# Attention scores of two heads in one go: cross terms over all rows, both high-high terms on half of the rows each

## The chip, the cores and the metric

The kernel runs on one core of a Trainium2 chip. The metric is device microseconds from start to end of one launch. The engines that appear below are PE (TensorE: matmuls; its weight loads are listed as PEld), DVE (VectorE), ACT (ScalarE), POOL (GpSimd) and SP (SyncE, which issues transfers). Matmuls write into PSUM, the accumulator memory, from which ACT and DVE read.

## What is computed

A residual block with masked self-attention in which queries, keys and values are the same projection: 16 batches, 512 channels, 1024 tokens, 8 heads of 64. About half of the tokens are masked out.

```python
def _L0_cond_ref(x, mask, Wq, Wo):
    NH = 8
    NEG = -1e+30
    B, D, T = x.shape
    dk = D // NH
    scale = 1.0 / jnp.sqrt(jnp.asarray(dk, x.dtype))
    xt = jnp.transpose(x, (0, 2, 1))
    q = xt @ Wq.T
    qh = q.reshape(B, T, NH, dk).transpose(0, 2, 1, 3)
    scores = scale * jnp.einsum('bhqd,bhkd->bhqk', qh, qh)
    cmask = mask[:, None, None, :]
    rmask = mask[:, None, :, None]
    logits = (scores * cmask + (1.0 - cmask) * NEG) * rmask
    attn = jax.nn.softmax(logits, axis=-1)
    ctx = jnp.einsum('bhqk,bhkd->bhqd', attn, qh)
    ctx = ctx.transpose(0, 2, 1, 3).reshape(B, T, D)
    out = ctx @ Wo.T
    return jnp.transpose(out, (0, 2, 1))
x = x + _L0_cond_ref(x, cond_2048, L0_cond_Wq, L0_cond_Wo)
```

## The kernel before

Only tokens with mask 1 attend and are attended to; the others get the mean. The kernel gathers the unmasked rows of a batch into C = 544 slots (four blocks of 128 and a tail of 32), works on those, and adds the mean's projection to the other rows.

**Numbers in two halves.** A float32 value is kept as h + l, two float16 numbers, h the rounded value and l the rest. The projections (`query`, L447, and `product`, L727) multiply h.h, h.l and l.h and leave l.l out. The scores need q.q within a head. `qsplit` makes, for each pair of heads, a tile `xx` of 128 partitions with four slots of 544 columns. For the pair's first head, slot 0 holds h in partitions 0 to 63 and l in 64 to 127, and slot 1 holds l and h, the other way round. For the second head, slot 2 holds h and l, and slot 3 l and h. A matmul of slot 0 with slot 0 over all 128 rows gives h.h + l.l at once, and one of slot 0 with slot 1 gives the two cross terms h.l + l.h. Four transfers on SP's queue fill `xx` (SP, "xx<-hl").

**Scores** (`scores`, L620). One call is one head `p` and one row block `i`: four matmuls into a tile `pss` of two PSUM banks, first h.h + l.l for both halves of the columns (g = 0, 1; 272 columns each), then the cross terms for both. One exp on ACT (L624) reads the tile into `p` and sums its rows (the accumulator is read by an instruction of its own). The pool `ps_s` has two such tiles. With `i` as None the tails of four heads are done together (L595), in four column groups of 32.

**Attend** (L643). exp(scores) times v, in float32, for both heads of a pair: the first head writes PSUM partitions 0 to 63, the second 64 to 127, so each matmul takes 64 columns of the array. The sixteen matmuls of a pair of heads for its four row blocks come as one block (32 records in the trace): the first is `group_first`, and the others are queued behind it with raised priority. The tail's part (L647) ends the sum, and ACT copies it out (L651).

**The order of the work.** `run` goes through the batches; a batch has 18 steps: 4 pairs of heads x 4 row blocks, and two steps for the tails. In a step the code issues the first head's scores, then planned work (`fill`, with a share of the batch's list by cost), then the second head's scores, then transfers and, at i = 1, the attend block of the pair before, then planned work again. The planned work belongs to the batches beside this one: transposes (`xt`, L424), queries (L447), values (L497), projections (L727), sums. Costs and shares are written by hand; at i = 0, 1, 2, 3 the shares before and after the second head are (1.0, 0.6), (0.1, 0.5), (0.9, 1.0), (0.9, 0.9). The code's order is a priority: the framework's scheduler issues, on each engine, what it takes to be ready, so an instruction can go ahead of one that waits. `behind(i)` puts what is written in it behind instruction `i` on its engine, and `high_priority` moves it up. The pool `ps_m` (tiles `pm`) has two buffers for everything but scores and attends.

**Beat.** `self.beat` is the last matmul of the latest scores or query; gathers and scatters on POOL (L339, L811) and some sums on DVE wait for it, so that they come at a steady pace. `self.exp` is the last exp; the sums over x on ACT are queued behind it.

Of the kernel before, what the change touches and what calls it, by code (L numbers as in the profile page):

```python
# [10 lines left out]
F32 = mybir.dt.float32  # L11
# [3 lines left out]
AF = mybir.ActivationFunctionType  # L15
# [4 lines left out]
P = 128  # L20
D = 512
T = 1024
H = 8
DK = 64
# [3 lines left out]
SCALE = 0.125  # L28
NEG = -1.0e30

C = 544
CT = C - 512
CH = C // 2
CQ = C + 2
CM = C
HG = H // 2
# [10 lines left out]
HPO = 300  # L47


class Fast:  # L50
# [531 lines left out]
    def scores(self, b, p, i):  # L582


        nc, s = self.nc, self.st[b]
        if "z" not in s:
            s["z"] = self.sb([P, H, 4], F32, "z", 2)
            s["zt"] = self.sb([P, 2], F32, "zt", 2)
        if i is None:
            pt = self.ps_s.tile([P, 2, 512], F32, tag="s", name="pss")  # L590
            for a in range(2):
                for g in range(2):
                    for r in range(HG):
                        xx, k = s["xx"][2 * p + r // 2], r % 2
                        self.beat = nc.tensor.matmul(pt[r * CT:(r + 1) * CT, g, :CH], lhsT=xx[:, 2 * k, 512:C],  # L595
                                                     rhs=xx[:, 2 * k + a, g * CH:(g + 1) * CH],
                                                     start=(a == 0), stop=(a == 1)).ins
            t = self.sb([P, C], F32, "p", 12)
            nc.scalar.activation(t.rearrange("p (g c) -> p g c", g=2), pt[:, :, :CH], AF.Exp,  # L599
                                 bias=s["nm"][p][:, HG:], scale=SCALE, accum_out=s["zt"][:, p:p + 1])  # L600

            hi = self.sb([P, C], F32R, "c", 4)
            lo = t.bitcast(F32R)
            nc.vector.tensor_copy(hi, t)
            nc.vector.tensor_tensor(lo, t, hi.bitcast(F32), ALU.subtract)  # L605

            def spread():
                s["pt"] = self.sb([P, 2, C], F32R, "pt")
                half = slice(0, DK), slice(DK, P)
                for k in range(2):  # L610
                    nc.sync.dma_start(out=s["pt"][half[k], k, :].bitcast(F32), in_=hi[half[k]].bitcast(F32))
                    nc.sync.dma_start(out=s["pt"][half[1 - k], k, :].bitcast(F32), in_=lo[half[k]].bitcast(F32))

            self.later(spread)
            return None
        xx, k = s["xx"][p // 2], p % 2
        pt = self.ps_s.tile([P, 2, 512], F32, tag="s", name="pss")
        for a in range(2):
            for g in range(2):
                self.beat = nc.tensor.matmul(pt[:, g, :CH], lhsT=xx[:, 2 * k, i * P:(i + 1) * P],  # L620
                                             rhs=xx[:, 2 * k + a, g * CH:(g + 1) * CH],
                                             start=(a == 0), stop=(a == 1)).ins
        t = self.sb([P, C], F32, "p", 12)
        self.exp = [nc.scalar.activation(t.rearrange("p (g c) -> p g c", g=2), pt[:, :, :CH], AF.Exp,  # L624
                                         bias=s["nm"][p // HG][:, p % HG:p % HG + 1], scale=SCALE,
                                         accum_out=s["z"][:, p, i:i + 1]).ins]
        return t

    def attend(self, b, p, i, ps):
        nc, s = self.nc, self.st[b]  # L630
# [214 lines left out]
    def run(self, flag):  # L845
# [24 lines left out]
        for i, e in enumerate(ends):  # L870
            g = list(range(ends[i - 1] + 1 if i else 0, e + 1))
# [73 lines left out]
        if True:  # L945
            for b in range(B + 1):
# [4 lines left out]
                free, sums, rows, third, tail, rest = {}, [], [], [], [], []  # L951
                if b:
                    sums, rows, third = [(0, L(self.recip_sums, o, 3))], [(0.1, L(self.recip_rows, o, 3))], [(0, L(self.norm, o, 3))]
# [11 lines left out]
                if n < B:  # L965
# [20 lines left out]
                    if b == 0:  # L986
                        k = next(k for k, (c, f) in enumerate(m) if f is index[0][1])
# [32 lines left out]
                def fill(part, end=False):  # L1020
                    nonlocal done, goal, pos
                    goal += part * unit
                    while pos < len(m) and (end or (part and done + m[pos][0] / 2 <= goal)):
                        m[pos][1]()
                        done += m[pos][0]
                        pos += 1

                for st, (p, i) in enumerate(S):
                    soon, self.soon = self.soon, []
                    for f in soon + free.get(st, []):  # L1030
                        f()
                    if i is None:
                        self.scores(b, p, None)
                    else:
                        ps = [self.scores(b, 2 * p, i)]
                        if i == 2 and whole:
                            whole.pop()()
                    fill(share[st][0], st == N - 1)
                    if i is not None:
                        ps.append(self.scores(b, 2 * p + 1, i))  # L1040

                    for _ in range(1 if b < B - 2 else -(-len(self.urgent + self.spare) // (N - st))):
                        self.issue()

                    if i == 0:
                        ready, todo = todo, []
                    elif i == 1:
                        self.group_first = None
                        for f in ready[3::-1] + ready[4:]:
                            f()  # L1050
                        ready = []
                    fill(share[st][1])
                    if i is not None:
                        todo.append(L(self.attend, b, p, i, ps))
                    if i == 3:
                        (whole if p < 3 else todo).append(L(self.attend, b, p, 4, None))
                        if p < 3:
                            free.setdefault(st + 2, []).append(L(self.recip_sums, b, p))
                            free.setdefault(st + 3, []).append(L(self.recip_rows, b, p))
                            if p < 2 or b == B - 1:  # L1060
                                free.setdefault(min(st + 7, N - 1), []).append(L(self.norm, b, p))
# [148 lines left out]
```

## Time and profile before

| | |
|---|---|
| three runs | 1061.43, 1064.06, 1066.17 us; median 1064.06 |
| span of the profiled execution | 1063.1 us |
| mean granted clock of PE | 0.992 |
| ACT, exp of the scores (L624) | 512 x 718 ns, and 512 accumulator reads of 203 ns |
| PE, weight loads for the scores (L620) | 2048 of 99 ns, beside the matmuls |
| PE, queries (L447), projections (L727) | six and three groups of 256 and 240 matmuls, 280 and 380 ns a record |

The profile is of one execution. A group's row gives its line, engine, operation, tiles, shape and count, then the busy time in us and the mean ns of one, then the engine's idle time ahead of the group and what ended most of it. For a matmul the shape is weights first (rows * columns of the array that are used), then the moving operand. Matmuls are pipelined: a record of a matmul with 272 columns is 0.28 us long, and the next one starts well before it ends, so the distance from start to start is the cost on PE. In the timeline, each row is a run of equal instructions: start, length of the run, engine, line, operation, tiles, shape and count, and in brackets the idle time ahead of it with what ended it.

### The profile page before, as it was taken

To read this page: it belongs to the slowest core of one execution; us is meant where nothing else is said; L and a number is where in the kernel's file an instruction comes from. 1 tells how busy PE (TensorE), PEld (TensorE's weight loads), DVE (VectorE), ACT (ScalarE), POOL (GpSimd) and SP (SyncE) were. 2 spreads that over 40 slices of the span, in tenths; PEclk is the share of its full clock that TensorE was granted. 3 is DMA by queue.
4 is the path that set the end of the run, shared out by engine and by line. 5 is a ranking of instruction groups with operands and counts; after the bars stand their busy time and mean duration, and the time that the engine had idled before them with its cause. 6 is when DMAs were issued, how large, how long until landed. Compare 5 with 4: busy or idle time off the path is not lost.

```text
span 1063.1 us, 23765 instructions
## 1 busy us (share of the span) xinstructions
PE 1021.6 (96%) x8626; PEld 701.6 (66%) x8626; DVE 729.2 (69%) x2376; ACT 672.5 (63%) x1722; POOL 298.6 (28%) x303
## 2 busy tenths in 40 slices
PE   7798999999999999999999999999999999999996
PEld 7576666666666767666676666767666676766553
DVE  6697668676766856776775766876676776666653
ACT  5876666666676766666676576676666676664550
POOL 3101013322301222332322223232232332235652
PEclk9899999999999999999999999999999999999998
DMA  6746555546654665766557575655856554575752
GB/s 206 226 132 166 136 166 165 177 142 204 174 145 137 160 189 156 195 194 165 173 149 210 167 199 172 162 166 148 239 174 179 170 159 144 142 195 170 222 172 76
DMA packets 78123, 181.37 MB, mean 171 GB/s; under 512 B 15008, under 2 KB 16800, under 8 KB 78000
## 3 DMA queue, kind: packets, MB, share of 16 engines
q1 hardware_dynamic: 56816, 111.62, 38.4%
q0 software_dynamic: 21184, 68.18, 20.5%
q8 instruction: 70, 1.15, 0.5%
q14 instruction: 53, 0.43, 0.1%
HBM read 92.34 MB, written 33.91 MB: 119 GB/s over the span
## 4 chain that ended last, share of the span: by engine, by line
PE 76%; ACT 10%; DVE 7%; issue 3%; DMA 2%; POOL 0%; POOLq 0%; DVEq 0%; SPq 0%; ACTq 0%
PE pav L643 22%; PE pss L620 17%; PE pm L727 15%; PE pm L447 12%; ACT p L624 5%; PE pm L424 2%; PE pav L647 2%; ACT xh L384 1%; DVE p L605 1%; ACT xm L369 1%; PE pss L595 1%; PE pm L497 1%; PE pm L680 1%; ACT v L500 1%; ACT p L599 1%
## 5 line engine op out<-in xcount | busy, mean ns | idle before, releaser
L624 ACT ACTIVATE p<-pss,nm 128x544 f32<-128x544 f32 x512 | 365.4, 718 | 217.5 <-PE pss L620 203.6
L620 PE MATMUL pss<-xx 128*128 128x272 f16 x2048 | 307.0, 280 | 6.5 <-ACT p L624 5.7
L643 PE MATMUL pav<-p,v 128*64 128x272 f32 x2048 | 248.8, 396 | 0.0
L620 PEld LDWEIGHTS <-xx 128*128 128x128 f16 x2048 | 194.7, 99 | 63.3 <-issue 22.5
L643 PEld LDWEIGHTS pav<-p,v 128*64 128x64 f32 x2048 | 141.4, 137 | 91.0 <-issue 13.9
L811 POOL DMA_INDIRECT y_out<-xa,idx x68 | 72.1, 1060 | 292.8 <-PE pss L620 150.2
L447 PE MATMUL pm<-xh,wqh 128*128 128x274 f16 (+1 forms) x512 | 143.9, 281 | 2.4 <-DVE xa L732 1.9
L447 PE MATMUL pm<-xh,wql 128*128 128x274 f16 (+1 forms) x512 | 143.2, 280 | 0.0
L447 PE MATMUL pm<-xl,wqh 128*128 128x274 f16 (+1 forms) x512 | 143.1, 280 | 0.0
L339 POOL DMA_INDIRECT xa<-x_in,idx x68 | 67.9, 999 | 210.6 <-PE pss L620 101.5
L447 PEld LDWEIGHTS <-wqh 128*128 128x128 f16 x1024 | 98.1, 99 | 25.8 <-issue 4.8
L624 ACT ACTIVATION_READ_ACCUMULATOR p<-pss,nm 128x1 f32 x512 | 104.0, 203 | 0.0
L811 POOL DMA_INDIRECT y_out<-xi,idx x60 | 69.5, 1159 | 107.5 <-PE pss L620 49.0
L727 PE MATMUL pm<-woh,ch 128*128 128x512 f16 x240 | 91.1, 380 | 0.0
L727 PE MATMUL pm<-woh,cl 128*128 128x512 f16 x240 | 90.9, 379 | 0.0
L727 PE MATMUL pm<-wol,ch 128*128 128x512 f16 x240 | 90.9, 379 | 0.0
L450 ACT ACTIVATE q<-pm 128x272 f32<-128x272 f32 (+1 forms) x128 | 50.9, 398 | 63.0 <-PE pm L447 62.8
L339 POOL DMA_INDIRECT xi<-x_in,idx x60 | 61.4, 1023 | 102.2 <-PE pss L620 43.5
L732 DVE SCALAR_TENSOR_TENSOR xa<-pm,xa 128x512 f32<-128x512 f32 x60 | 41.3, 688 | 63.3 <-PE pm L727 59.9
L727 PEld LDWEIGHTS <-ch 128*128 128x128 f16 x480 | 45.6, 98 | 45.9 <-issue 1.4
L798 DVE TENSOR_TENSOR xi<-xi,ub 128x512 f32<-128x512 f32 (+1 forms) x60 | 40.9, 688 | 42.6 <-PE pss L620 42.0
L711 DVE TENSOR_TENSOR c<-c,rb 128x544 f32<-128x544 f32 x64 | 46.2, 722 | 28.0 <-PE pm L447 17.1
(194 smaller groups left out, 1558.4 us busy)
## 6 DMA issues: line engine op xcount, KB each, us to landing
xx<-hl SPq DMA_DIRECT2D x256, 136.0 KB
xm<-x_nat_in SPq DMA_DIRECT2D x56, 512.0 KB
rb<-rd SPq DMA_DIRECT2D x128, 136.0 KB
pt<-c SPq DMA_DIRECT2D x64, 136.0 KB
pt<-p SPq DMA_DIRECT2D x64, 136.0 KB
ub<-ud SPq DMA_DIRECT2D x16, 256.0 KB
xi<-x_nat_in SPq DMA_DIRECT2D x8, 256.0 KB
xa<-x_in,idx POOLq DMA_INDIRECT x68, 4.6
```

Source lines behind the costliest of these rows:

```text
L339: dma = self.nc.gpsimd.indirect_dma_start(out=tile[:n], out_offset=None, in_=self.x, in_offset=bass.IndirectOffsetOnAxis(ap=idx, axis=0))
L424: self.pe = nc.tensor.transpose(pt[:, c, :], x[:n, c * P:(c + 1) * P], self.ident[:n, :n]).ins
L447: self.beat = nc.tensor.matmul(pq, lhsT=w[:, c, e * P:(e + 1) * P], rhs=xx[:, c, cols], start=(k == 0), stop=(k == 3 * DC - 1)).ins
L450: nc.scalar.activation(s["q"][:, e, cols], pq, AF.Copy, scale=1.0 / (SX * SW))
L620: self.beat = nc.tensor.matmul(pt[:, g, :CH], lhsT=xx[:, 2 * k, i * P:(i + 1) * P], rhs=xx[:, 2 * k + a, g * CH:(g + 1) * CH], start=(a == ...
L624: self.exp = [nc.scalar.activation(t.rearrange("p (g c) -> p g c", g=2), pt[:, :, :CH], AF.Exp, bias=s["nm"][p // HG][:, p % HG:p % HG + 1 ...
L643: mm = nc.tensor.matmul(s["pav"][k * DK:(k + 1) * DK, g, :CH], lhsT=s["v"][p][:, i, k * DK:(k + 1) * DK], rhs=ps[k][:, cols], start=(i == ...
L711: self.once(nc.vector.tensor_tensor(c, c, s["rb"][p], ALU.mult), self.beat if p < 3 else None)
L727: nc.tensor.matmul(po[:cols.stop - cols.start], lhsT=a[:, e, cols], rhs=w[:, e, :], start=(e == 0 and k == 0), stop=(e == DC - 1 and k == 2))
L732: self.nc.vector.scalar_tensor_tensor(x, po, 1.0 / (SX * SW), x, ALU.mult, ALU.add)
L798: self.once(self.nc.vector.tensor_tensor(x[:n], x[:n], s["ub"][:n], ALU.add), self.beat)
L811: dma = self.nc.gpsimd.indirect_dma_start(out=self.out, out_offset=bass.IndirectOffsetOnAxis(ap=idx, axis=0), in_=x, in_offset=None)
```

## The change

`scores` keeps only the tails. A new function `pair` does both heads of a pair for one row block: it takes both PSUM tiles, issues the cross terms of the first head and then of the second over all 128 rows (four matmuls, which now start the sums), and then the h.h terms, four matmuls over 64 rows each: the first head's h from partitions 0 to 63 of slot 0, the second head's from partitions 64 to 127 of slot 3. These alternate between the heads for each half of the columns, each is queued behind the one before and has raised priority. The l.l terms are left out. Then both exps follow. The step in `run` calls `pair` where the first head's scores stood, and the second head's place, behind the planned work, is empty.

```diff
-        xx, k = s["xx"][p // 2], p % 2
-        pt = self.ps_s.tile([P, 2, 512], F32, tag="s", name="pss")
-        for a in range(2):
+        assert False
+
+    def pair(self, b, p, i):
...
+        xx = s["xx"][p]
+        rows = slice(i * P, (i + 1) * P)
+        pts = []
+        for k in range(2):
+            pt = self.ps_s.tile([P, 2, 512], F32, tag="s", name="pss")
             for g in range(2):
-                self.beat = nc.tensor.matmul(pt[:, g, :CH], lhsT=xx[:, 2 * k, i * P:(i + 1) * P],
-                                             rhs=xx[:, 2 * k + a, g * CH:(g + 1) * CH],
-                                             start=(a == 0), stop=(a == 1)).ins
-        t = self.sb([P, C], F32, "p", 12)
-        self.exp = [nc.scalar.activation(t.rearrange("p (g c) -> p g c", g=2), pt[:, :, :CH], AF.Exp,
-                                         bias=s["nm"][p // HG][:, p % HG:p % HG + 1], scale=SCALE,
-                                         accum_out=s["z"][:, p, i:i + 1]).ins]
-        return t
+                mm = nc.tensor.matmul(pt[:, g, :CH], lhsT=xx[:, 2 * k, rows], rhs=xx[:, 2 * k + 1, g * CH:(g + 1) * CH],
+                                      start=True, stop=False)
+            pts.append(pt)
+        for g in range(2):
+            for k in range(2):
+                h = xx[k * DK:(k + 1) * DK, 3 * k, :]
+                with self.behind(mm.ins), self.tc.high_priority(offset=HPO):
+                    mm = nc.tensor.matmul(pts[k][:, g, :CH], lhsT=h[:, rows], rhs=h[:, g * CH:(g + 1) * CH],
+                                          start=False, stop=True)
+        self.beat = mm.ins
+        ps = []
+        for k in range(2):
+            t = self.sb([P, C], F32, "p", 12)
+            self.exp = [nc.scalar.activation(t.rearrange("p (g c) -> p g c", g=2), pts[k][:, :, :CH], AF.Exp,
+                                             bias=s["nm"][p // 2][:, p % 2 * 2 + k:p % 2 * 2 + k + 1], scale=SCALE,
+                                             accum_out=s["z"][:, 2 * p + k, i:i + 1]).ins]
+            ps.append(t)
+        return ps
...
-                        ps = [self.scores(b, 2 * p, i)]
+                        ps = self.pair(b, p, i)
                         if i == 2 and whole:
                             whole.pop()()
                     fill(share[st][0], st == N - 1)
-                    if i is not None:
-                        ps.append(self.scores(b, 2 * p + 1, i))
-
```

More of the change, by code (lines that the diff above doesn't have):

```diff
@@ L615, in scores @@
             return None
-        xx, k = s["xx"][p // 2], p % 2
-        pt = self.ps_s.tile([P, 2, 512], F32, tag="s", name="pss")
-        for a in range(2):
-            for g in range(2):
-                self.beat = nc.tensor.matmul(pt[:, g, :CH], lhsT=xx[:, 2 * k, i * P:(i + 1) * P],
-                                             rhs=xx[:, 2 * k + a, g * CH:(g + 1) * CH],
-                                             start=(a == 0), stop=(a == 1)).ins
-        t = self.sb([P, C], F32, "p", 12)
-        self.exp = [nc.scalar.activation(t.rearrange("p (g c) -> p g c", g=2), pt[:, :, :CH], AF.Exp,
-                                         bias=s["nm"][p // HG][:, p % HG:p % HG + 1], scale=SCALE,
-                                         accum_out=s["z"][:, p, i:i + 1]).ins]
-        return t
+        assert False
+    def pair(self, b, p, i):
+        nc, s = self.nc, self.st[b]
+        if "z" not in s:
+            s["z"] = self.sb([P, H, 4], F32, "z", 2)
+            s["zt"] = self.sb([P, 2], F32, "zt", 2)
+        xx = s["xx"][p]
[3 more added lines that the diff above has]
+            pt = self.ps_s.tile([P, 2, 512], F32, tag="s", name="pss")
+            for g in range(2):
+                mm = nc.tensor.matmul(pt[:, g, :CH], lhsT=xx[:, 2 * k, rows], rhs=xx[:, 2 * k + 1, g * CH:(g + 1) * CH],
[16 more added lines that the diff above has]
+        return ps
     def attend(self, b, p, i, ps):
```

## The prediction

> **What bounds the kernel now.** I read the page's first parts, then the groups by line, then stretches of the timeline in which TensorE (PE) changes the shape of its tiles, and last the waits. The page:
>
> ```profile
> PE 1021.6 (96%) x8626; PEld 701.6 (66%) x8626; DVE 729.2 (69%) x2376; ACT 672.5 (63%) x1722; POOL 298.6 (28%) x303
> ...
> PE 76%; ACT 10%; DVE 7%; issue 3%; DMA 2%; POOL 0%; POOLq 0%; DVEq 0%; SPq 0%; ACTq 0%
> ...
> L624 ACT ACTIVATE p<-pss,nm 128x544 f32<-128x544 f32 x512 | 365.4, 718 | 217.5 <-PE pss L620 203.6
> L620 PE MATMUL pss<-xx 128*128 128x272 f16 x2048 | 307.0, 280 | 6.5 <-ACT p L624 5.7
> L643 PE MATMUL pav<-p,v 128*64 128x272 f32 x2048 | 248.8, 396 | 0.0
> ```
>
> PE is busy for 96% of the span and makes 76% of the chain that ended last; no other engine is above 69%. So each ns taken from PE's stream counts, and each ns in which PE stands still counts as much. The scores (L620) are 2048 matmuls, 8 for each of 256 steps (16 batches, 4 pairs of heads, 4 row blocks). A mean of 280 ns is a record's length, which overlaps the next; the pitch is what counts, and it is read where only the scores run:
>
> ```profile
> 509.07 1.09 PE L620 MATMUL pss<-xx 128*128 128x272 f16 x8
> 510.09 3.89 PE L643 MATMUL pav<-p,v 128*64 128x272 f32 x32
> 513.91 1.10 PE L620 MATMUL pss<-xx 128*128 128x272 f16 x8
> 514.85 0.28 PE L447 MATMUL pm<-xh,wqh 128*128 128x272 f16 x1
> ```
>
> Eight matmuls last 1.09 us, the last record 0.28 of it, so the pitch is (1.09 - 0.28) / 7 = 0.116 us. The same lines show what a change of tile shape costs. The eight started at 509.07 and the next instruction of the same shape would start at 509.07 + 8 x 0.116 = 510.00; the first 64-column one starts at 510.09. Smaller windows around f16 work, and around the one place that uses fewer rows:
>
> ```profile
> 523.02 0.38 PE L727 MATMUL pm<-woh,cl 128*128 128x512 f16 x1
> 523.33 0.65 PE L595 MATMUL pss<-xx 128*32 128x272 f16 x16
> 523.91 0.33 PE L549 MATMUL pm<-ident,smcol 128*128 128x128 f32 x1
> ...
> 547.80 0.65 PE L595 MATMUL pss<-xx 128*32 128x272 f16 x16
> 548.38 0.43 PE L424 MATMUL pm<-ident,xt 32*128 32x32 f32 x4
> 548.75 0.41 PE L620 MATMUL pss<-xx 128*128 128x272 f16 x2
> ```
>
> A 512-column matmul has a pitch of 0.216 us (L727's starts in a row, 522.81 and 523.02), so L595 should start at 523.24; it starts at 523.33: 0.093 us go into the change. Sixteen L595 matmuls lie in four columns of 32: 0.65 us from the first start to the last end, of which the last record is 0.28, so 0.37 us from the first start to the last: three rounds of four, 3 x 0.116, and about 0.02 for the first weights and the small steps within a round. Four matmuls side by side take one pitch. The way out costs the same: the fourth round starts 0.37 after 523.33, at 523.70, and would be done at 523.81; L549 starts at 523.91. L424's tile of 32 rows follows columns directly, and is followed by full tiles, with gaps of the same size. So a change of shape costs 0.093 to 0.095 us each time, for rows and for columns, and the next weights are loaded in the open, 0.01 us for f16.
>
> **The change, part by part.** Times are on PE, per step of a pair of heads.
>
> Removed: the four matmuls of h.h + l.l (two halves of the columns for each head), 4 x 0.116 = 0.464 us.
>
> Kept: four cross matmuls, 0.464 us, only moved: the second head's stand right behind the first's.
>
> Added: four matmuls over 64 rows each, which are meant to run two at a time. Change into the tiles 0.093, open weights 0.010, two rounds 2 x 0.116 = 0.232, the second tile's start 0.004, change back 0.094, open weights 0.010: 0.443 us. Their weight loads stay four and cost nothing else: L497's 64-column f16 matmuls, each with a 128x128 load of its own, follow one another at 0.029 us, so four loads fit behind two rounds; uncovered they would be 4 x 0.029 = 0.12 us.
>
> Sum: 0.443 - 0.464 = -0.021 us a step, x 256 = **-5.4 us**. Half the matmul rounds go, 2 x 0.116 x 256 = 59 us, and the two changes of shape take 54 of them back.
>
> One change less: in 62 of the 64 blocks of L643 the instruction before it is a score. Where the half-row matmuls are last there, the way out and L643's way in are one change, about 0.10 us less: between 0 and 64 x 0.10 = 6.4 us. I take half, **-3.2 us**, because planned work that stood between the two heads now comes behind the pair and can fall between it and the block.
>
> Not shown by the trace: two half-row tiles at once. Bounds: side by side as the columns of L595 and L643 are (0 more), or one after another (2 x 0.116 x 256 = 59 us more). I take 0, the nearest row: L643's pairs and L595's fours lose nothing but the start. The Trainium skill, "TensorE: Matmul & The Clock Gate", Part 3 (Packing small matmuls), gives 3.07 times for four row tiles, not 4; by that share, 0.77, two tiles would give 1.53 times and a round 0.151 us, an estimate of 2 x 0.035 x 256 = 18 us more in all and 1091.5 us for the kernel, which is a part of rival (2) below. No row here has row tiles side by side to set beside it.
>
> The waits: before, the first head's scores, planned work, the second head's scores, planned work; each tile of scores (two buffers) had to wait for an exp that began a good half step earlier. Now both tiles finish with the last half-row matmul, both exps start then, and the next step needs both buffers at once. In the timeline:
>
> ```profile
> 490.32 0.63 PE L620 MATMUL pss<-xx 128*128 128x272 f16 x4
> 490.78 0.27 PE L549 MATMUL pm<-ident,smcol 128*128 128x128 f32 x1
> 490.89 0.63 PE L620 MATMUL pss<-xx 128*128 128x272 f16 x4
> 492.00 0.28 PE L620 MATMUL pss<-xx 128*128 128x272 f16 x1 [0.48 <-ACT p L624]
> 492.11 0.36 PE L558 MATMUL pm<-ident,m 128*128 128x4 f32 x2
> ...
> 491.14 0.71 ACT L624 ACTIVATE p<-pss,nm 128x544 f32<-128x544 f32 x1
> 491.74 0.21 ACT L624 ACTIVATION_READ_ACCUMULATOR p<-pss,nm 128x1 f32 x1
> 491.83 0.72 ACT L624 ACTIVATE p<-pss,nm 128x544 f32<-128x544 f32 x1
> ```
>
> The exp at 491.14 ends at 491.85, and PE goes on at 492.00: 0.15 us for the release. A second exp starts 0.69 after the first. So behind the last half-row matmul: its record 0.28, start of the exp 0.04, 0.69, 0.72, release 0.15 = 1.88 us until the second buffer is free. The next step's second head is reached one pitch and two cross matmuls later, 0.35 us. PE therefore needs 1.88 - 0.35 = 1.53 us of other work between two pairs, if ACT has nothing else ahead. I counted from the timeline, for the 239 steps behind the first batch, how long PE now spends between the scores of a step and those of the next, both stretches (behind the first and behind the second head) together: mean 2.89 us, but under 1.53 in 55 steps, which lack 31 us in all. ACT has 203 us of other work (672.5 - 365.4 - 104.0 for the accumulator reads), 0.8 us a step; with 0.7 of that ahead of the exps, PE would need 2.2 us, 82 steps lack it, 76 us in all. On the other side, work that is ready is issued ahead of what is not: only one of the four scores that start at 492.00 goes then, and L558 and a whole query follow it, so the order is the scheduler's and not the code's, and a short gap can be filled from a long one. The present waits for a free tile, 58 starts with 15 us together by their lost pitch, could go too. Bounds -15 and +76; I take **+18 us**, a little over half of the 31, since the mean gap has room but planned work comes in pieces of 1.4 (a query, 12 x 0.116) and 2.6 us (a projection, 12 x 0.216) and ACT is not free. Behind a waiting score on PE stand the attends and queries of all later steps, so every such wait is lost.
>
> DVE, POOL and the queues get no instruction more. Gathers and scatters wait for the last score (the beat), now that of the pair, at most 0.5 us later; POOL is busy 28% and has no share in the chain, so 0. Were that cover gone, it would be 0.5 us at a transfer, not per step. Both exps behind one another also hold up ACT's copies of queries, by up to 0.7 us; two buffers of pm cover that, and the range holds it if not.
>
> Sum: -5.4 - 3.2 + 18 = **+9.4 us**. The profiled execution's span of 1063.1 becomes 1072.5; the median of the runs shown lies 1.0 us above that span, so 1073.5.
>
> **Rivals.** (1) Fewer rounds, and no new waits: the scheduler fills every short gap and 3 of the 15 us of present waits vanish. For it: the mean gap of 2.89 us is nearly twice the 1.53 needed. Against it: the scheduler does not prevent 58 waits today, with half the coupling. Time 1064.1 - 5.4 - 3.2 - 3 = 1052.5, faster. It decides once the new waits are under 9 us. (2) The half-row matmuls do not run at once, so that the change does not do what it says: 1073.5 + 59 = 1133; half overlapped 1103. For it: no row shows it; against it: L595. (3) This change of shape is cheaper than the columns' one: without both drains, 1073.5 - 256 x 0.207 = 1020.5. Against it: L424's rows, priced like columns. (4) ACT's other work stands ahead of the exps everywhere: 1064.1 - 8.6 + 76 = 1131.5. Against it: the scheduler reorders.
>
> **How the numbers follow.** Forecast 0.42, (1) 0.30, (2) 0.15 (none and half overlap about alike), (3) 0.07, (4) 0.06. The forecast's own range is 1062 to 1092, waits of 7 to 37 us. Half of a per cent, 5.3 us, is about what this measurement can tell from no change. Faster (under 1058.7): most of (1), (3) and a little of the forecast, 0.35. Within: 0.15, the low end of the forecast and the high end of (1). Slower: the rest, 0.50. The range leaves out (3) below, and (4) and the whole of no overlap above: 1045 to 1112.
>
> **What would show it.** In the changed trace: second half-row matmul of a round some 0.004 us behind the first, rounds 0.116 apart (overlap); 0.21 us from the last cross matmul to the first half-row one and from the last half-row one to the next instruction (drains); PE's waits for ACT's exp grown from 5.7 us of idle by 10 or more. The forecast is wrong if that row stays under 9 us, or if the starts within a round are 0.1 us apart.

## The result, and the profile after

The changed kernel takes 1077.88 us (median of 4 runs, 1076.47 to 1084.01), the kernel before 1064.07 us beside it: a ratio of 1.0143, 95% interval 1.0116 to 1.0169. It is 13.8 us slower; 9.4 us had been forecast, inside a range of 1045 to 1112. The profiled execution has a span of 1075.1 us, 12.0 more than before.

The page of the changed kernel (lines L630 and L637 are the cross terms and the half-row matmuls, L643 the exp, L664 the attend):

```profile
PE 1023.9 (95%) x8626; PEld 619.9 (58%) x8626; DVE 739.0 (69%) x2376; ACT 670.9 (62%) x1722; POOL 308.1 (29%) x303
...
PE 71%; DVE 11%; ACT 10%; issue 4%; DMA 3%; SPq 0%; POOL 0%; POOLq 0%; DVEq 0%; ACTq 0%
...
L643 ACT ACTIVATE p<-pss,nm 128x544 f32<-128x544 f32 x512 | 361.2, 711 | 188.6 <-PE pss L637 186.1
L664 PE MATMUL pav<-p,v 128*64 128x272 f32 x2048 | 248.8, 396 | 0.0
...
L630 PE MATMUL pss<-xx 128*128 128x272 f16 x1024 | 178.1, 279 | 15.8 <-ACT p L643 15.0
...
L637 PE MATMUL pss<-xx 64*128 64x272 f16 x1024 | 103.8, 281 | 0.0
```

The busy time of the scores fell from 307.0 to 178.1 + 103.8 = 281.9 us, and yet PE as a whole is busy as long as before, 1023.9 against 1021.6. A record is 0.28 us long where the next matmul can start after 0.116, so a start that comes up to 0.16 us late leaves no gap between the records: this row cannot show what a change of shape costs. The starts can. The timeline of PE at two steps of the changed kernel (start, length of the run, line, tiles, shape, count):

```profile
509.19 0.63 PE L630 MATMUL pss<-xx 128*128 128x272 f16 x4
509.75 0.41 PE L637 MATMUL pss<-xx 64*128 64x272 f16 x4
510.08 0.77 PE L668 MATMUL pav<-pt,vt 128*128 128x272 f32 x4
...
517.29 0.63 PE L630 MATMUL pss<-xx 128*128 128x272 f16 x4
517.85 0.41 PE L637 MATMUL pss<-xx 64*128 64x272 f16 x4
518.18 0.91 PE L664 MATMUL pav<-p,v 128*64 128x272 f32 x6
```

Four full-row matmuls last 0.63 us, the last record 0.28 of it: three pitches. Four half-row ones last 0.41: 0.13 us from the first start to the last, one pitch and two small steps, so two run at a time. The cross terms would be done with their pitch at 509.19 + 4 x 0.116 = 509.65, and the half rows start at 509.75, 0.10 later. The last half-row start is at 509.88, and the next instruction comes at 510.08, 0.20 later, where 0.116 is the pitch. Over all steps the median distances are 0.211 us into the half rows, 0.003 within a round, 0.123 from round to round, 0.207 out of them.

PE's waits, longest first (engine, line, waited for: us in all, times, longest), in the changed kernel:

```profile
PE pss L630 <- ACT p L643: 15.0, 28, 1.0
PE pm L190 <- DVE mh L177: 3.5, 1, 3.5
PE pss L424 <- DMA xa<-x_in,idx: 3.3, 1, 3.3
PE pss L595 <- DMA xx<-hl: 2.6, 2, 2.2
PE pss L595 <- ACT p L643: 2.5, 3, 1.3
...
PE pm L701 <- DVE rcol L695: 0.6, 1, 0.6
```

In the kernel before, the rows for the exp and for the reciprocal's transpose (L701, there L680) were:

```profile
PE pm L680 <- DVE rcol L674: 6.3, 9, 0.7
PE pss L620 <- ACT p L624: 5.7, 13, 0.7
```

One of the longest waits for the exp in the changed kernel, with ACT's rows below PE's:

```profile
497.98 0.64 PE L630 MATMUL pss<-xx 128*128 128x272 f16 x4
498.55 0.41 PE L637 MATMUL pss<-xx 64*128 64x272 f16 x4
498.88 0.33 PE L549 MATMUL pm<-ident,smcol 128*128 128x128 f32 x1
500.24 0.39 PE L630 MATMUL pss<-xx 128*128 128x272 f16 x2 [1.03 <-ACT p L643]
...
498.06 1.05 ACT L369 ACTIVATE xm<-xm 128x1024 f32<-128x1024 f32 x1
499.01 0.20 ACT L369 ACTIVATION_READ_ACCUMULATOR xm<-xm 128x1 f32 x1
499.10 0.39 ACT L450 ACTIVATE q<-pm 128x274 f32<-128x274 f32 x1
499.38 0.72 ACT L643 ACTIVATE p<-pss,nm 128x544 f32<-128x544 f32 x1
499.98 0.21 ACT L643 ACTIVATION_READ_ACCUMULATOR p<-pss,nm 128x1 f32 x1
500.07 0.72 ACT L643 ACTIVATE p<-pss,nm 128x544 f32<-128x544 f32 x1
```

Both scores tiles are full at 498.96. PE has one transpose to do until the next pair, and that pair needs the buffer whose exp ends at 500.10. PE goes on at 500.24. ACT was held by a sum over x and a copy, and the exps started 0.42 us late.

The waits are not spread evenly over the steps. Of the 15.0 us, 6.2 come in six waits of 1.03 us like this one, each behind a transpose of L549, and 5.2 in twelve waits between the first and the second head's cross terms, where one scores tile is free and the other is not. In the kernel before, scores started 0.11 to 0.17 us behind L549 in 30 of its 32 places, as at 490.89 in the prediction's timeline. From L549's starts to the next ones PE spent 4.2 us in all before, and spends 18.0 now.

To see all of PE's time at once I went through its matmuls from start to start and split each distance into three: up to the pitch of the matmul (for float16 on full tiles a straight line through the two measured pitches, 0.116 us for 272 columns and 0.216 for 512; the measured pitch of its group for float32 and small tiles) it is work; where the next instruction has another tile shape, up to 0.107 us more is the change, a bound set a little above the 0.08 to 0.10 read above; the rest is standing still. Where the lines are drawn is a choice: other pitches for the float32 and small tiles move some us between work and standing still. The sum of a row does not depend on it.

| us, from the first matmul's start to the last's | work | changes of shape (count) | standing still | all |
|---|---|---|---|---|
| before | 956.0 | 21.9 (225) | 72.7 | 1050.6 |
| changed | 906.4 | 67.8 (712) | 88.7 | 1062.8 |
| difference | -49.6 | +45.9 (+487) | +16.0 | +12.2 |

### The profile page after: what moved, and what is told of

It reads as the page before. It is cut to its first block, busy times and chain, and to the rows that moved or that the text cites. A ratio compares the mean times of both kernels' runs of the same rounds, so it can differ in the third digit from the quotient of the medians.

```text
span 1075.1 us, 23760 instructions
## 1 busy us (share of the span) xinstructions
PE 1023.9 (95%) x8626; PEld 619.9 (58%) x8626; DVE 739.0 (69%) x2376; ACT 670.9 (62%) x1722; POOL 308.1 (29%) x303
## 4 chain that ended last, share of the span: by engine, by line
PE 71%; DVE 11%; ACT 10%; issue 4%; DMA 3%; SPq 0%; POOL 0%; POOLq 0%; DVEq 0%; ACTq 0%
PE pav L664 22%; PE pm L447 13%; PE pm L748 12%; PE pss L630 8%; ACT p L643 6%; PE pss L637 6%; PE pm L424 3%; PE pav L668 3%; PE pss L595 1%; DVE sd L485 1%; ACT xm L369 1%; DVE tmp L484 1%; PE pm L701 1%; DMA xx<-hl 1%; DVE xa L753 1%
## 5 line engine op out<-in xcount | busy, mean ns | idle before, releaser
L643 ACT ACTIVATE p<-pss,nm 128x544 f32<-128x544 f32 x512 | 361.2, 711 | 188.6 <-PE pss L637 186.1
L664 PE MATMUL pav<-p,v 128*64 128x272 f32 x2048 | 248.8, 396 | 0.0
L664 PEld LDWEIGHTS pav<-p,v 128*64 128x64 f32 x2048 | 141.3, 137 | 91.0 <-issue 13.9
L630 PE MATMUL pss<-xx 128*128 128x272 f16 x1024 | 178.1, 279 | 15.8 <-ACT p L643 15.0
L832 POOL DMA_INDIRECT y_out<-xa,idx x68 | 72.2, 1062 | 308.7 <-DVE xa L753 121.7
L447 PE MATMUL pm<-xh,wqh 128*128 128x274 f16 (+1 forms) x512 | 144.1, 281 | 4.3 <-DVE xa L753 1.9
L447 PE MATMUL pm<-xl,wqh 128*128 128x274 f16 (+1 forms) x512 | 143.1, 280 | 0.2 <-DVE xl L385 0.2
L447 PE MATMUL pm<-xh,wql 128*128 128x274 f16 (+1 forms) x512 | 143.2, 280 | 0.0
L630 PEld LDWEIGHTS <-xx 128*128 128x128 f16 x1024 | 98.3, 101 | 56.4 <-issue 33.4
L339 POOL DMA_INDIRECT xa<-x_in,idx x68 | 72.9, 1072 | 176.5 <-PE pss L637 61.8
L447 PEld LDWEIGHTS <-wqh 128*128 128x128 f16 x1024 | 94.8, 99 | 37.4 <-issue 20.3
L637 PE MATMUL pss<-xx 64*128 64x272 f16 x1024 | 103.8, 281 | 0.0
L643 ACT ACTIVATION_READ_ACCUMULATOR p<-pss,nm 128x1 f32 x512 | 101.8, 199 | 0.0
L748 PEld LDWEIGHTS <-ch 128*128 128x128 f16 x480 | 42.8, 98 | 49.0 <-issue 9.2
```

The lines of the kernel that those rows point to most:

```text
L339: dma = self.nc.gpsimd.indirect_dma_start(out=tile[:n], out_offset=None, in_=self.x, in_offset=bass.IndirectOffsetOnAxis(ap=idx, axis=0))
L447: self.beat = nc.tensor.matmul(pq, lhsT=w[:, c, e * P:(e + 1) * P], rhs=xx[:, c, cols], start=(k == 0), stop=(k == 3 * DC - 1)).ins
L630: mm = nc.tensor.matmul(pt[:, g, :CH], lhsT=xx[:, 2 * k, rows], rhs=xx[:, 2 * k + 1, g * CH:(g + 1) * CH], start=True, stop=False)
L637: mm = nc.tensor.matmul(pts[k][:, g, :CH], lhsT=h[:, rows], rhs=h[:, g * CH:(g + 1) * CH], start=False, stop=True)
L664: mm = nc.tensor.matmul(s["pav"][k * DK:(k + 1) * DK, g, :CH], lhsT=s["v"][p][:, i, k * DK:(k + 1) * DK], rhs=ps[k][:, cols], start=(i == ...
L748: nc.tensor.matmul(po[:cols.stop - cols.start], lhsT=a[:, e, cols], rhs=w[:, e, :], start=(e == 0 and k == 0), stop=(e == DC - 1 and k == 2))
```

## Experiments

The runs below were made on four different chips, and the kernel before took 1062 to 1074 us on them. So each result stands as a ratio to the kernel before on the same chip. The changed kernel was measured three times: 1.0143 (above), and on two of the chips below, 1.0115 and 1.0126. The variant with full rows came out at 1.0143 on one chip and 1.0183 on another, 4 us apart, so a comparison across chips is good to about that; one on the same chip is better.

**The pair alone, with full rows.** Everything as in the changed kernel, but h.h + l.l over all 128 rows, as before the change: eight rounds and no half rows.

```diff
-                h = xx[k * DK:(k + 1) * DK, 3 * k, :]
+                h = xx[:, 2 * k, :]
```

> The changed order, both heads together, but h.h + l.l over all 128 rows as before: eight rounds, no change of shape. Theory (bringing the pair together costs PE 16 us of waits by itself): about 1064 + 16 = 1080 us, PE's idle ahead of scores waiting for the exp near the 15 us of the changed kernel. Rival (the waits come with the half-row matmuls, which are held up between the cross terms and the exp): 1064 us, idle near the 5.7 us of before.

Measured: 1089.46 us against 1073.88, ratio 1.0143 (1.0126 to 1.016). Slower by as much as the changed kernel, with no half-row matmul in it. Since the two ran on different chips, both were run again in the same rounds:

> The changed kernel beside its variant with full rows, on one chip and in the same rounds, since the two had been measured on different chips. Theory (the half rows are worth 5 us on PE, the pairing costs 15): 5 us under the variant, ratio to the kernel before 1.010 to 1.014. Rival (the half rows give nothing at all): within 2 us of the variant.

> The pair of heads with h.h + l.l over all rows once more, beside the changed kernel. Theory: ratio to the kernel before 1.014 to 1.018 and 5 us over the changed kernel; the whole of it comes from the pairing. Rival: the same time as the changed kernel within 2 us.

Measured on one chip: before 1062.37, changed 1075.77 (ratio 1.0126, 1.0108 to 1.0145), pair with full rows 1081.61 (1.0183, 1.0168 to 1.0199). Bringing the heads together costs 19.2 us by itself on this chip; the half rows then bring back 5.8. By starts, the full-row variant of this chip has 956.7 us of work, 23.0 of changes and 87.6 standing, and the changed kernel 906.5, 67.8 and 88.4: 50.2 us less work for 44.8 us more changes, and the same standing, which is 15 to 16 us more in both than the 72.7 of the kernel before on the first chip. The rows of the two, changed kernel first (L637 holds full rows in the second):

```profile
L630 PE MATMUL pss<-xx 128*128 128x272 f16 x1024 | 178.2, 279 | 15.8 <-ACT p L643 15.4
L637 PE MATMUL pss<-xx 64*128 64x272 f16 x1024 | 103.8, 281 | 0.0
```

```profile
L630 PE MATMUL pss<-xx 128*128 128x272 f16 x1024 | 177.7, 279 | 16.6 <-ACT p L643 14.9 <-issue 0.3
L637 PE MATMUL pss<-xx 128*128 128x272 f16 x1024 | 160.8, 279 | 0.0
```

The wait for the exp is 15 us with half rows and with full rows, so the half rows have no part in it.

**Six rounds without a change of shape.** The second head's h.h is left out, and all six rounds use 128 rows.

```diff
-                                      start=True, stop=False)
+                                      start=True, stop=(k == 1))
...
         for g in range(2):
-            for k in range(2):
-                h = xx[k * DK:(k + 1) * DK, 3 * k, :]
-                with self.behind(mm.ins), self.tc.high_priority(offset=HPO):
-                    mm = nc.tensor.matmul(pts[k][:, g, :CH], lhsT=h[:, rows], rhs=h[:, g * CH:(g + 1) * CH],
-                                          start=False, stop=True)
+            h = xx[:, 0, :]
+            with self.behind(mm.ins), self.tc.high_priority(offset=HPO):
+                mm = nc.tensor.matmul(pts[0][:, g, :CH], lhsT=h[:, rows], rhs=h[:, g * CH:(g + 1) * CH],
+                                      start=False, stop=True)
```

> Six rounds as in the changed kernel, but all of them over 128 rows: h.h + l.l for the first head alone, the second head's h.h is left out. Theory (two changes of shape a step cost PE 0.21 us each step, in the open): 1078 - 0.21 x 256 = 1024 us if the waits stay, up to 1035 if they grow. Rival (the drains lie in time that PE would wait anyway): above 1055.

Measured: 1045.16 us against 1073.88, ratio 0.9732 (0.9708 to 0.9756). With the changed kernel's 1.012 to 1.014 that is about 42 us for the two changes of a step, across chips, where 43 to 54 had been counted. By starts, the changes fell by 43 us (24.5 against 67.7 in the changed kernel's second run, the one beside the two trips below), and standing grew by 11 (107.0 against 95.6): the price of the changes of shape is real, and a part of what is saved goes into waits. In the rows of waits, the scores' wait for ACT's exp grew by 2.1 us to 14.2, and L558's for DVE by 3.7 to 5.8.

**Both heads on the same rows.** All half-row matmuls use rows 0 to 63, so that none can run beside another if it is the different rows that let two overlap.

```diff
-                h = xx[k * DK:(k + 1) * DK, 3 * k, :]
+                h = xx[:DK, 2 * k, :]
```

> Both heads' h.h on the same half of the rows (0 to 63; the second head's h is there too, in slot 2), so that they can't run at once; nothing else differs. Theory (half-row matmuls on different rows overlap fully, PE is the bound): two rounds more, 2 x 0.116 x 256 = 59 us more, 1137 us, starts in the group 0.116 us apart. Rival (the overlap is partial, or covered by waits): under 1115.

Measured: 1126.6 us, ratio 1.049 (1.0465 to 1.0516), 37 to 40 us over the changed kernel (by its ratio of 1.012 to 1.014) where 59 had been expected. In time alone that is near the rival's 1115 us: 1.049 is 1116 us on the chip of the first result. The starts decide. The timeline of PE in this run:

```profile
515.92 0.63 PE L637 MATMUL pss<-xx 64*128 64x272 f16 x4
516.48 0.77 PE L668 MATMUL pav<-pt,vt 128*128 128x272 f32 x4
```

Four in 0.63 us, like full rows, where the changed kernel had 0.41. The work by starts is 965.6 us, 59 more than the changed kernel's 906.6, just as counted; standing is 81.7 us, against 95.6 in the changed kernel's second run. So the overlap of two row tiles is complete but for 0.003 us and worth 59 us on PE. The time moved by less because PE stood still for less; 4 us of that lie in the scores' row of waits for the exp (8.2 against 12.1), which a longer score section covers in part, and where the rest lies was not followed up.

**Two trips into the half rows.** First the cross terms of one half of the columns, their h.h, then the other half.

```diff
...
+            if g == 0:
+                for k in range(2):
+                    with self.behind(mm.ins), self.tc.high_priority(offset=HPO):
+                        mm = nc.tensor.matmul(pts[k][:, 1, :CH], lhsT=xx[:, 2 * k, rows], rhs=xx[:, 2 * k + 1, CH:C],
+                                              start=True, stop=False)
```

> The changed kernel once more, beside the other three, so that they have it on the same chip: the ratio to the kernel before stays near 1.014, as the first measurement had it, by every theory. A ratio under 1.005 or over 1.025 would say that the loss hangs on the chip.

> The same matmuls as in the changed kernel, but the half-row ones in two trips, one for each half of the columns with the full-row cross terms between: four changes of shape a step instead of two. Theory (each trip costs PE 0.21 us in the open): 0.21 x 256 = 54 us more than the changed kernel. Rival (a share of it is taken out of the waits for the exp): 30 to 45 us more, as two more rounds gave 37 where 59 were counted.

Measured on one chip: before 1073.12, changed 1084.42 (ratio 1.0115, 1.0087 to 1.0142), two trips 1136.18 (1.0592, 1.0557 to 1.0627). That is 51.8 us for 256 more trips, 0.20 us each, near the theory's 54 and above the rival's 30 to 45: doubling the suspected cost adds it once more.

**Half of the exp.** Exps of 272 columns instead of 544, the attends read the first half twice, the sums get a higher floor, and their correction is added instead of subtracted. The second half of the weights is left out.

```diff
-            self.exp = [nc.scalar.activation(t.rearrange("p (g c) -> p g c", g=2), pts[k][:, :, :CH], AF.Exp,
+            self.exp = [nc.scalar.activation(t[:, :CH], pts[k][:, 0, :CH], AF.Exp,
...
-                                              rhs=ps[k][:, cols], start=(i == 3), stop=False)
+                                              rhs=ps[k][:, :CH], start=(i == 3), stop=False)
...
```

> The changed kernel with exps over half of the columns (272 of 544), used by the attend matmuls for both halves; the sums' floor is raised so that the numbers stay finite. The second half of the weights is left out, PE's matmuls are the same in number and size. Theory (the new waits are those for the two exps behind one another): about 0.36 us less for each exp, the waits for the exp fall by 15 us or more, 12 to 20 us under the changed kernel. Rival (the scheduler's order, or pm and DVE, hold PE up): under 6 us less.

Measured, on the chip of the two trips: 1067.09 us, ratio 0.9953 (0.9936 to 0.997), 17.3 us under the changed kernel with the same number and size of matmuls. And the same edit on the kernel before, on another chip:

> The kernel before, with exps over half of the columns and the attends and floor as in the other half-exp run; the second half of the weights is left out. Theory (the waits of the changed kernel come from having both heads' exps between two pairs; before, most exps are covered): 3 to 8 us under the kernel before, since only its 15 us of waits for a free tile can shrink. Rival (shorter exps help any order alike, so that the 17 us of the other run say nothing on the pairing): 14 to 20 us under it.

Measured: 1066.87 us against 1072.69, ratio 0.9951 (0.9936 to 0.9966), 5.8 us. The scores of the changed kernel on that first chip, with full exps and with half exps:

```profile
L630 PE MATMUL pss<-xx 128*128 128x272 f16 x1024 | 178.4, 279 | 18.2 <-ACT p L643 12.1 <-issue 3.3 <-ACT q L450 2.1
L630 PE MATMUL pss<-xx 128*128 128x272 f16 x1024 | 176.5, 279 | 10.9 <-ACT p L643 6.7 <-issue 1.5 <-ACT p L599 0.8
```

And those of the kernel before with half exps:

```profile
L620 PE MATMUL pss<-xx 128*128 128x272 f16 x2048 | 306.1, 280 | 2.9 <-ACT p L624 2.5 <-issue 0.2
```

With short exps the two orders take the same time (0.9953 and 0.9951, on two chips), although the paired one still waits longer. What the change loses hangs on the length of the exp. The row of waits for the exp shows only a part of it: it fell by 5.4 us, where 15 or more had been expected, and all idle time ahead of L630 by 7.3; the rest of the 17.3 us is spread over other rows. Of the two kinds of waits, those between the two heads' cross terms (4.7 us for the exp with full exps on this chip) are gone, and those of scores behind L549 stay (6.3 us with full exps, 6.0 with half ones).

**More even stretches between the pairs.** The planned work's shares:

```diff
-                share = [(1.2, 0) if i is None else ((1.0, 0.6), (0.1, 0.5), (0.9, 1.0), (0.9, 0.9))[i] for _, i in S]
+                share = [(1.2, 0) if i is None else ((1.0, 1.0), (0.0, 0.0), (1.0, 0.9), (1.0, 1.0))[i] for _, i in S]
```

> The changed kernel with planned work shared so that the stretches behind the pairs at i = 0, 2, 3 get equal parts (2.0 each, none at i = 1, where the attend block stands). Theory (the new waits come from short stretches between two pairs): the waits for the exp fall by half or more, 1065 to 1072 us. Rival (other work of ACT ahead of the exps, or the scheduler's own order, sets them): 1078 us within 4.

Measured: 1095.04 us against 1073.88, ratio 1.0191 (1.0158 to 1.0224), against 1.0115 to 1.0143 for the changed kernel on other chips: no gain, and probably a loss. PE's wait for the exp was 14.4 us in 33 waits: the waits moved, and standing still was 106.8 us. The theory failed, and the rival, no difference within 4 us, is not borne out either. The shares are given by hand-written costs in pieces of up to 2.6, and the scheduler moves ready work past a waiting pair anyway, so equal shares on paper need not be equal stretches on PE; which of the two was at work was not tried.

**ACT's sums over x at other steps.** The long wait shown above has a sum of 1.05 us ahead of the exps, so the sums were queued behind the exps of i = 1, where the attend block follows.

```diff
-                        at = 3 * c + (0 if b else 4)
+                        at = 3 * c + 4 if b == 0 else (0, 2, 4, 8)[c]
                         free.setdefault(at, []).append(L(self.load_all, b + 2, c, None if b else first_top))
-                        free.setdefault(at + 4, []).append(L(self.sum_half, b + 2, c))
+                        free.setdefault(at + 4 if b == 0 else (3, 7, 11, 16)[c], []).append(L(self.sum_half, b + 2, c))
```

> The changed kernel with ACT's four sums over x in each batch (1.05 us each) queued behind the exps of i = 1, where the attend block of 3.8 us follows, instead of steps 4, 7, 10, 13; the loads for them are moved along. Theory (a part of the new waits is ACT's other work standing ahead of the paired exps; the 1.25 us waits have such a sum ahead of them): 3 to 8 us less than the changed kernel. Rival (only the length of the two exps counts): within 2 us of the changed kernel.

> The kernel before with ACT's sums over x moved as in the run on the changed kernel. If those 8 us more were the new places of the sums and loads as such: 4 to 10 us slower than before here too. If they came of the paired order alone: within 2 us of before.

Measured: on the changed kernel 1092.76 us, ratio 1.0192 (1.0166 to 1.0219), 8.3 us slower than without the edit on the same chip. On the kernel before 1075.62 against 1072.69, ratio 1.0024 (1.0014 to 1.0035), 2.9 us slower, between the two expectations. The theory that the sums ahead of the exps make the waits failed: the wait for the exp stayed at 12.6 us (12.1 without the edit), and the wait for a scores tile without a releaser in the profile ("issue") grew from 3.3 to 8.2. The sum in the example lengthened that one wait, but where the sums stand is not what the 15 us hang on. Why the new places are worse, and more so in the paired order, stays open.

## Why the prediction was right, step by step

**PE's sum.** Forecast: two rounds less and two changes more a step, -5.4 us, and one change less at the attend blocks, -3.2: -8.6 together. Shown: 5.8 us between the changed kernel and its full-row variant on one chip, which holds both. The mechanism is as forecast: the change of shape for rows costs what it did for columns (0.211 us into the half rows and 0.207 out, against 0.210 with the pitch), two row tiles overlap (starts 0.003 us apart; 59 us of work come back when both use the same rows), and 256 more trips cost 0.20 us each where 0.21 was counted. The gain is 3 us smaller than forecast, for the reasons under "The work".

**The unseen overlap.** I took the columns' rows as the nearest and the bound of 0. That held, and the Trainium skill's 3.07 times for four row tiles ("TensorE: Matmul & The Clock Gate", Part 3), which would have made 18 us more of it, does not describe this case: the rounds are 0.123 us apart, not 0.151. The 4 ns that the same part of the Trainium skill gives between the starts of tiles agree with the 0.003 us here.

**One change less.** -3.2 us was forecast, half of 64 places. The count of changes rose by 487, not 512: 25 fewer, 2.6 us. In 34 of the 64 attend blocks the half rows stand right ahead; in 23 others the scheduler put the block between the first and the second head's cross terms.

**The work.** -59 us of rounds and +6 of open weights and small steps were counted, -53; the starts show -49.6. Two terms were sized too small. The rounds are 0.123 us apart instead of 0.116, 1.8 us in 256 steps. And the next instruction after the half rows is a float32 one on full tiles in 107 of 256 steps (L668 in 55), where 0.010 us of open weights had been counted, the float16 price. From the last half-row start to L668's second matmul PE needs 0.437 us (0.206 and 0.231). In the kernel before, and in the variant with full rows, it was 0.241 (0.028 and 0.213) from the last score. That is 0.196 us more, where 0.104 was counted: 5 us too little in 55 steps. The other changes came out 0.01 us cheaper than counted, which gives some of it back.

**The waits.** +18 us was taken between -15 and +76; standing still rose by 16.0 us in the first profile and by 15 in the pair with full rows, whose time rose by 19.2. That they come with the pairing and not with the half rows is shown by that variant, and that they hang on the exp's length by the half exps (17.3 us against 5.8 before the change). The mark set for the row of waits for ACT's exp was missed by a little: 5.7 to 15.0 us is 9.3 more, not 10. The rest of the new standing sits ahead of transposes and queries (L424 up 4 us, L447 up 4, by starts), while one old wait shrank (for the reciprocal's transpose, 9.5 to 1.1). So the mechanism is shown, but that the sum came so near to 18 is in part luck: the 18 was chosen inside wide bounds and for the scores' waits alone, and the 16 is their rise, other rises that were not counted and a fall of 8 us that was not foreseen.

**The way from there to the total.** -5.4 - 3.2 + 18 = +9.4 was forecast, +11.3 to +13.8 came in three measurements. By starts, PE's own part is -49.6 + 45.9 = -3.7 us instead of -8.6, and the waits are 16.0 instead of 18: +12.2. In the first measurement the runs' median rose a little more than the profiled span. The first rival, that ready work fills every short stretch, falls with the 15 us; the second and third with the starts; the fourth with the sum of 16 us instead of 76. How my bound of 31 us, from stretches under 1.53 us, became 15 is not resolved: the scheduler's order differs between the two kernels, and the experiments that were to steer it (shares, sums) did not make it better. A kernel with the paired order and more than two scores tiles was not tried.

No run of the full computation beat the kernel before.

## What to carry to other kernels

Two matmuls over 64 rows each ran here in the time of one, but a trip into another tile shape cost PE about 0.2 us in the open, some two pitches of 272 columns; count trips against rounds saved, and go only where one trip holds many rounds. Look at what follows the trip, too: a float32 matmul on full tiles behind it cost 0.05 to 0.10 us more than a float16 one. Where two heads share two PSUM tiles, issuing both at once gives up the double buffering: price the reader's time between two pairs, not only the matmuls. When a change has two parts, make the variant with one of them first; here the order alone cost more than the whole change.

## What was not expected of the hardware

Lengthening PE's work by 59 us cost about 39, and taking out 43 us of changes of shape and 9 of work gained about 42, with 11 us more standing: on this stream, which is 95% busy, a part of each of these changes was covered by less standing still, or lost to more of it. The same kernel before took 1062 us on one chip and 1074 on another, 1.1% apart; most of the single differences looked for here are smaller than that.
